# The turn from layer 0 to attention: tile 24's heads behind layer 0's last product, tile 25's in one piece, and the edge sums' bank emptied into a buffer of its own

## The chip, the core and the metric

One core of a Trainium2 chip. The metric is the device time of the whole program in microseconds (us), as the median of several runs. A second source is one profiled execution, read as a page and through questions to its trace. The engines are named as the profile names them: PE (TensorE's matmuls), PEld (its weight loads), DVE (VectorE), ACT (ScalarE), POOL (GpSimd), SP (SyncE, which issues most DMAs).

## What is computed

Two layers over a graph of 3327 nodes with 1024 features, in float32.

```python
# layer 0
h = max(layernorm(x), 0)
s = act_quant(relu(act_quant(h) @ weight_quant(w)))          # 4 bits
x = x + adj @ s                                               # scaled by asf and the quantisation steps
# layer 1
h = max(layernorm(x), 0)
Wh = einsum('nf,hfd->hnd', h, W)                              # 8 heads of 64
e = leaky_relu(Wh @ a1 [:, None] + Wh @ a2 [None, :], 0.2)
att = softmax(where(adj > 0, e, -9e15))
h = elu(att @ Wh)                                             # heads side by side: 512
out = relu(relu(relu(h @ W1.T + b1) @ W2.T + b2) @ W3.T + b3) @ W4.T + b4
x = x + out
```

## The kernel before

The nodes are padded to T = 26 tiles of 128 rows. Layer 0's second product (`mm`, line 726) takes each tile t of rows in four parts of 7, 6, 7 and 6 column blocks; every block of the adjacency is split into a high and a low float32r half (`hi` by ACT, line 185; `lo` by DVE, line 189) and multiplied with the resident quantised support `s_int[j]`. After a tile's product comes its chain: `y` (ACT, line 742; DVE, 744), `xt` = x + y (745), the row statistics (141 to 146), the ReLU of the centred row into `y` (144), its transpose into `ht`, and the inverse root `r` (`half_inverse`, lines 131 to 134, and 755).

`heads(t, ht, r)` makes layer 1's features of a tile: eight float32 products with `whead` (638; the profile counts 16 instructions), the scaled copy `wht` (ACT, 645), two products and reductions for `src` and `dst` (DVE, 652 and 653), exponentials on ACT (657, 676), the scaled features `ft` (DVE, 677), their high and low halves `fw` (ACT 692, DVE 693) and the halves `dw` that the edge sums use (ACT, 697). POOL stores them to `feat_d` (701) and `dsum_d` (705). In some tiles (`BATCHES`) the `src` rows gathered so far are transposed into the bank `sp` (661), copied (665) and stored to `src_d` (668). Heads of tile t - 1 are placed ahead of the last part of tile t's product. Tile t < 25 is transposed by DMA (`transposed_by_dma`, lines 607 to 612: two copies, two DMA transposes, two copies into `ht`); the last by TensorE (`transposed_by_tensor`, 626 and 627). With `own` given, `heads` also writes the first head's features straight into the attention's resident buffers `f_even` and `dw` (689, 691).

Attention sums over neighbours by two kinds of product. For each of 32 `attends` (column half, head pair, head, block group) and each of 26 neighbour tiles j, DVE makes a 0/1 selection `sel` (1063) of six or seven 128x128 blocks (which edges are on the positive side of the leaky ReLU), and PE adds `sel` times features into as many accumulator banks (`acc`, 1077). The second kind, the edge sums (`mps`, 852), multiplies the mask of one block (cast by ACT to `mf`, 13 tiles at a time, 849) with `dw` over all 26 tiles, in one bank, which ACT copies to `part` (856). `n` counts the pairs of attend and j; `edge_steps(n)` says how many edge products are done by then: before, none until n = 12, 24 at n = 14, all 338 of the first pair at n = 62.

The instructions of each engine run in the order that a scheduler lays down from priorities and estimated times. Three means fix it where wanted: `issue_after(ins)` puts a block's instructions of the same engine behind `ins`; `queue_behind(a, b)` puts a behind b; neither adds a wait. `keep_in_program_order` ties an instruction to the order of the source. Memory is reused: the eight PSUM banks of layer 0 (`mm` 4, `whm` 2, `sp` 1, `last` 1) become seven `acc` banks and one `mps` bank; the mask, features and `dw` of the attention lie where `s_int` lay, and its `sel`, `mf` and `srow` where `at`, `mk`, `hi` and `lo` lay.

The turn, as the trace before shows it: heads of tile 24 on PE from 899.4 to 906.1 us, the last 24 `mm` products to 912.13, then products of attend 0 for j = 0 to 3, the eight transposes of tile 25 (from 917.88), then tile 25's heads with one `acc` step (seven products) after each of their eight products (to 934.0), the transpose of `src`, 26 edge products, and the attention's steady order from about 950.

Of the kernel before, what the change touches and what calls it, by code (L numbers as in the profile page):

```python
# [8 lines left out]
F32 = mybir.dt.float32  # L9
# [36 lines left out]
BATCHES = {12: 0, T - 3: 13, T - 1: T - 2}  # L46
# [15 lines left out]
def two_layer_kernel(  # L62
# [105 lines left out]
    with tc.tile_pool(name="at", bufs=2, reuse_waits="tile") as atp:  # L168
# [419 lines left out]
        with tc.tile_pool(name="wh", bufs=1, reuse_waits="tile") as whp, tc.tile_pool(  # L588
# [31 lines left out]
            def transposed_by_tensor(y):  # L620
                ht = s2.tile([P, KF, P], F32, name="ht", bufs=1)
                for g in range(KF // 4):
                    tp = last_ps.tile([P, 4, P], F32, tag="last", name="tp2")
                    for q in range(4):
                        k = 4 * g + q
                        nc.tensor.transpose(tp[:, q, :], y[:, k * P : (k + 1) * P], ident)
                    last = nc.scalar.copy(ht[:, 4 * g : 4 * g + 4, :], tp)
                return ht, last

            def heads(t, ht, r, own=None):  # L630
                if t == T - 1:
                    whm, sp = (last_ps.tile([P, EMB], F32, tag="last", name=n) for n in ("whm", "sp"))
                else:
                    whm = wh_ps.tile([P, EMB], F32, name="whm")
                    sp = sp_ps.tile([P, EMB], F32, name="sp")
                of_k, products = [], []
# [9 lines left out]
                if t < T - 1:  # L646
# [10 lines left out]
                nc.scalar.activation(ratio[:, t], src, AF.Exp, scale=1.0 - SLOPE)  # L657
                if t in BATCHES:
                    first = BATCHES[t]
# [15 lines left out]
                for q, slope in enumerate((1.0, SLOPE)):  # L675
                    exps = nc.scalar.activation(ft[:, :, q, HD], dst, AF.Exp, scale=slope)
# [5 lines left out]
                if own is not None:  # L682
# [5 lines left out]
                    for up, value in zip(ups, values):  # L688
                        nc.scalar.copy(up, value)
                    for up, down, value in zip(ups, downs, values):  # L690
                        scaled = nc.vector.tensor_tensor(down, value, up.bitcast(F32), ALU.subtract)
                nc.scalar.copy(fw[:, :, 0], f2)
# [16 lines left out]
                return of_k, products, lows, exps, scaled, taken  # L709

            before = None
            for t in range(T):
# [5 lines left out]
                for js in PARTS:  # L718
                    hi, lo = part
                    part = next(columns, None)  # L720
                    if js is PARTS[-1] and before is not None:
                        _, products, lows, exps, made, _ = heads(*before)
# [18 lines left out]
                with tc.issue_after(exps.ins) if t == T - 1 else nullcontext():  # L741
                    nc.scalar.activation(y, mm, AF.Copy, scale=r_asf)
                with tc.issue_after(made.ins) if t == T - 1 else nullcontext():
# [499 lines left out]
```

## Time and profile before

| | us |
|---|---|
| Median of 3 runs | 2217.43 (2217.34 to 2218.85) |
| The profiled execution's own time | 2215.07 |
| Its span, first to last instruction | 2213.2 |
| PE busy | 2175.8 (98%) |
| DVE busy | 1541.5 (70%) |
| ACT busy | 1114.6 (50%) |
| Mean granted TensorE clock | 0.999 |

An instruction row gives start, duration, engine, line, operation, output and inputs, count, and in brackets the idle time of its engine before it with what ended that wait. A windows row gives the stretch, its length, the busy time of each engine with the number of instructions, the granted clock of TensorE (1.00 is full), the share of the DMA engines in use and the rate in GB/s. Of a duration of several matmuls in a row, the end is modelled.

### The profile page before, as it was taken

The numbers are of one execution on the slowest core, as the hardware profiler recorded it, in microseconds if no ns is written. First come the engines' busy times: TensorE is split into PE (matmuls) and PEld (weight loads), VectorE is DVE, ScalarE is ACT, GpSimd is POOL, SyncE is SP. The second block draws the span as 40 slices with busy tenths as digits, with TensorE's granted clock in tenths as the row PEclk, the third lists the DMA queues.
The fourth block names the chain that finished last, engine by engine and source line by source line (L and its number), as shares of the span: only waits on it lengthen the run. The fifth ranks groups of instructions, "written<-read, shape, count | busy, mean of one in ns | idle before, by whom it ended". The sixth has DMA issues, their size and how long they took to land.

```text
span 2213.2 us, 31276 instructions
## 1 busy us (share of the span) xinstructions
PE 2175.8 (98%) x12447; PEld 1749.6 (79%) x12457; DVE 1541.5 (70%) x1998; ACT 1114.6 (50%) x1714; POOL 176.8 (8%) x269
## 2 busy tenths in 40 slices
PE   5999999999999999999999999999999999999999
PEld 2477777777777777699999999999999999744444
DVE  8745555555455555678999999999999999822211
ACT  6734444544455544466556566565555555532110
POOL 2301000112001111000000000000000000000000
PEclk9999999999999999999999999999999999999999
DMA  6654566655556555934242432654242432372221
GB/s 219 166 185 156 158 189 184 177 166 158 182 185 185 168 168 160 332 117 149 87 148 80 132 101 60 217 162 145 87 150 87 138 90 78 100 205 92 95 86 67
DMA packets 242722, 321.40 MB, mean 145 GB/s; under 512 B 104901, under 2 KB 187285, under 8 KB 242577
## 3 DMA queue, kind: packets, MB, share of 16 engines
q1 hardware_dynamic: 221964, 246.18, 36.7%
q0 software_dynamic: 20544, 73.18, 10.5%
q8 instruction: 97, 1.59, 0.3%
q14 instruction: 49, 0.39, 0.1%
q10 hardware_dynamic: 68, 0.06, 0.0%
HBM read 208.99 MB, written 86.79 MB: 134 GB/s over the span
## 4 chain that ended last, share of the span: by engine, by line
PE 94%; DVE 3%; DMA 2%; ACT 1%; issue 1%; SPq 0%; POOL 0%; DVEq 0%; ACTq 0%; POOLq 0%
PE acc L1077 29%; PE mm L726 27%; PE mps L852 15%; PE whm L638 8%; PE o L1158 8%; PE h_ps L1118 5%; PE mm L337 2%; DMA xqt<-xq 0%; DVE stats L250 0%; DMA w<-in_w 0%; DVE sel L1063 0%; PE h_ps L1027 0%; PE o_half L1158 0%; DMA at<-in_adj_t 0%; DMA yht<-yh 0%
## 5 line engine op out<-in xcount | busy, mean ns | idle before, releaser
L1063 DVE SCALAR_TENSOR_TENSOR sel<-srow,ndst,mask 128x896 fp32r<-128x896 f32 (+1 forms) x832 | 864.0, 1078 | 51.6 <-PE acc L1077 40.2
L852 PE MATMUL mps<-dw,mf 128*128 128x260 f32 x2704 | 452.8, 283 | 0.3 <-ACT srct L665 0.3
L726 PE MATMUL mm<-s_int,hi 128*128 128x512 f32 x1352 | 426.7, 397 | 0.0
L726 PE MATMUL mm<-s_int,lo 128*128 128x512 f32 x1352 | 416.5, 389 | 0.0
L1077 PE MATMUL acc<-f_even,sel 128*128 128x260 f32 x2704 | 401.0, 286 | 2.9 <-DVE sel L1063 2.1
L1077 PE MATMUL acc<-f_odd,sel 128*128 128x260 f32 x2704 | 394.1, 286 | 0.4 <-DVE sel L1063 0.4
L849 ACT CAST mf<-mask 128x1664 fp32r<-128x1664 uint8 x208 | 331.3, 1593 | 118.8 <-PE mps L852 95.1
L852 PEld LDWEIGHTS mps<-dw,mf 128*128 128x128 f32 x2704 | 377.2, 188 | 1.1 <-ACT srct L665 0.6
L1077 PEld LDWEIGHTS acc<-f_even,sel 128*128 128x128 f32 x2704 | 356.8, 189 | 9.8 <-issue 3.6
L1077 PEld LDWEIGHTS acc<-f_odd,sel 128*128 128x128 f32 x2704 | 352.7, 188 | 7.9 <-issue 2.6
L726 PEld LDWEIGHTS mm<-s_int,hi 128*128 128x128 f32 x1352 | 254.0, 188 | 62.9 <-issue 12.0
L726 PEld LDWEIGHTS mm<-s_int,lo 128*128 128x128 f32 x1352 | 253.7, 188 | 52.8
L189 DVE TENSOR_TENSOR lo<-at,hi 128x896 fp32r<-128x896 f32 x104 | 106.2, 1021 | 130.4 <-ACT hi L185 130.2
L638 PE MATMUL whm<-whead,ht 128*128 128x512 f32 x416 | 183.8, 592 | 0.0
L1158 PE MATMUL o<-weights,h 128*128 128x512 f32 x400 | 174.8, 592 | 0.0
L190 DVE TENSOR_SCALAR mk<-at 128x896 uint8<-128x896 f32 (+1 forms) x104 | 61.5, 593 | 142.5 <-DMA at<-in_adj_t 142.5
L185 ACT CAST hi<-at 128x896 fp32r<-128x896 f32 x104 | 92.2, 887 | 134.7 <-PE mm L726 96.0
L1158 PEld LDWEIGHTS o<-weights,h 128*128 128x128 f32 x400 | 76.0, 190 | 94.4 <-issue 94.0
L638 PEld LDWEIGHTS whm<-whead,ht 128*128 128x128 f32 x416 | 78.3, 189 | 85.7 <-issue 83.5
L856 ACT COPY part<-mps 128x260 f32<-128x260 f32 x104 | 39.4, 379 | 188.4 <-PE mps L852 188.4
L921 POOL DMA_DIRECT2D enc_d<-eh x64 | 57.5, 903 | 934.2 <-ACT eh L919 933.7
L1128 ACT ACTIVATE h<-h_ps,rest 128x512 f32<-128x512 f32 (+1 forms) x54 | 34.8, 654 | 179.4 <-PE h_ps L1118 179.4
(169 smaller groups left out, 1674.1 us busy)
## 6 DMA issues: line engine op xcount, KB each, us to landing
feat_d<-fw POOLq DMA_DIRECT2D x26, 1040.0 KB, 5.4
f_even<-feat_d SPq DMA_DIRECT2D x7, 3380.0 KB, 13.5
f_odd<-feat_d SPq DMA_DIRECT2D x7, 3380.0 KB, 13.3
at<-in_adj_t SPq DMA_DIRECT2D x52, 448.0 KB, 4.4
at<-in_adj_t SPq DMA_DIRECT2D x52, 384.0 KB, 4.1
dw<-dsum_d SPq DMA_DIRECT2D x16, 910.0 KB, 9.2
dsum_d<-dw POOLq DMA_DIRECT2D x26, 520.0 KB, 6.4
x_d<-xt POOLq DMA_DIRECT2D x26, 512.0 KB, 6.7
```

The lines of the kernel that those rows point to most:

```text
L185: ins = nc.scalar.copy(hi, at)
L189: nc.vector.tensor_tensor(lo, at, hi.bitcast(F32), ALU.subtract)
L190: ins = nc.vector.tensor_scalar(mk[:, r], at, 0.0, None, ALU.is_gt)
L638: ins = nc.tensor.matmul(whm, ht[:, k, :], whead[:, k, :], start=(k == 0), stop=(k == KF - 1))
L726: nc.tensor.matmul(mm[:, c * 512 : (c + 1) * 512], which[:, q, :], s_int[j][:, c * 512 : (c + 1) * 512], start=(j == 0 and which is hi), s ...
L849: ins = nc.scalar.copy(mf, mask[:, j : j + TH, :])
L852: nc.tensor.matmul(ps, mf[:, j % TH, :], dw[:, j, :], start=(j == 0), stop=(j == T - 1))
L921: nc.gpsimd.dma_start(enc_d[q, sub[0] * P : (sub[-1] + 1) * P, h * HD : (h + 1) * HD].rearrange("(b p) d -> p b d", p=P), eh[:, q].rearran ...
L1063: ins = nc.vector.scalar_tensor_tensor(sel[:, :nb], srow[:, :nb], ndst[:, j, h : h + 1], mask[:, :, j, :], ALU.is_gt, ALU.mult,)
L1077: ins = nc.tensor.matmul(accs[b], sel[:, b, :], f[:, j, :], start=(j == 0), stop=(j == T - 1))
L1118: ins = nc.tensor.matmul(pss[m][:, :cols], wt[:, k, m * P : (m + 1) * P], xt[:, k, :cols], start=(k == 0), stop=(k == k_n - 1),)
L1158: nc.tensor.matmul(ps, h3[:, k, q * P : (q + 1) * P], w4[:, k, cs], start=(k == 0), stop=(k == D3 // P - 1),)
```

## The change

- Layer 0's last tile no longer has heads in front of its last part. `heads(24)` is called after the loop, with `own` buffers as `heads(25)` has; its products come after the last `mm` products, and its first DVE product and `wht` behind the end of tile 25's inverse root (`lacking`).
- Tile 25's two groups of transposes come behind the heads of tile 24, with attend 0's j = 0 between the groups and j = 1 to 3 behind the second; then all heads of tile 25 in one piece, then j = 4 to 7, then the edge products.
- On DVE `sel` 0 to 3 stand ahead of tile 25's y (`resumed`), 4 to 7 behind tile 24's scaled features, then tile 24's low halves, then tile 25's products; `sel` from 8 stands behind tile 25's scaled features.
- The edge sums begin at n = 7 with 24 steps at once and go on evenly from n = 9; the 338 are still reached at n = 62.
- The first edge block's bank is copied to `kept`, and from there to `part` before block 1's copy; the high copy `fw` of tile 25 stands behind that copy and behind the second mask cast of block 1.
- The `src` rows of tiles 24 and 25 are transposed in `last_src`, in the `mps` bank, after edge block 4.
- On SP the first half of the mask of group 0 and `srow` go ahead of the last DMA transpose of tile 24 (`turned`); the features and `dw` of tiles 20 to 23 go ahead of mask 1, tile 24 is no longer loaded for head 0.

```diff
-BATCHES = {12: 0, T - 3: 13, T - 1: T - 2}
+BATCHES = {12: 0, T - 3: 13}
...
             def transposed_by_tensor(y):
...
+                ends, copies = [], []
                 for g in range(KF // 4):
                     tp = last_ps.tile([P, 4, P], F32, tag="last", name="tp2")
...
+                    turns = [
+                        nc.tensor.transpose(tp[:, q, :], y[:, (4 * g + q) * P : (4 * g + q + 1) * P], ident)
+                        for q in range(4)
+                    ]
+                    ends.append((turns[0], turns[-1]))
+                    copies.append(nc.scalar.copy(ht[:, 4 * g : 4 * g + 4, :], tp))
+                return ht, ends, copies
...
-                    if js is PARTS[-1] and before is not None:
-                        _, products, lows, exps, made, _ = heads(*before)
+                    if js is PARTS[-1] and before is not None and t < T - 1:
+                        heads(*before)
...
+                resumed = nc.vector.tensor_scalar(y, y, asf_t, sup_delta, ALU.mult, ALU.mult)
...
+                lacking = nc.vector.tensor_scalar(r, r, 2.0, None, ALU.mult)
+                if t == T - 1:
+                    break
+                ht, turned = transposed_by_dma(y)
...
-            last_heads, *_, scaled, taken = heads(*before, own=(f_even, dw))
+            kept = large(early, "kept", [P, 2, 2 * HC])
+
+            of_k, products, lows, powers, scaled, own_lows, _, _, taken = heads(*before, own=(f_even, dw))
+            queue_behind(products[0], lacking)
+            queue_behind(taken, lacking)
+            ht, turns, copies = transposed_by_tensor(y)
+            queue_behind(turns[0][0], of_k[-1])
+            queue_behind(copies[0], taken)
+            queue_behind(powers[0], copies[-1])
+            last = heads(T - 1, ht, r, own=(f_even, dw))
+            queue_behind(last[1][0], lows)
...
-    FIRST = 12
+    FIRST = 7
...
-    YOUNG = 14
+    YOUNG = 9
...
+        def last_src():
+
+            first = max(BATCHES) + 1
+            n = (T - first) * NH
+            sp = m_ps.tile([P, 512], F32, tag="mps", name="sp2")
+            nc.tensor.transpose(sp[:n, :P], srcs[:, first:].rearrange("p t h -> p (t h)"), ident)
+            srct = s3.tile([P, P], F32, name="srct2")
+            nc.scalar.copy(srct[:n], sp[:n, :P])
...
+                            behind = nullcontext()
+                            if u == 0 and i * T + j <= T:
+                                behind = tc.issue_after((last[6] if i else powers)[-1].ins)
+                            with behind:
                                 ins = nc.scalar.copy(mf, mask[:, j : j + TH, :])
                             if amid:
-                                queue_behind(taken, ins)
+                                queue_behind(last[-1], ins)
+                            elif (u, i, j) == (0, 1, TH):
+                                queue_behind(last[7], ins)
...
+                            if u == i == 0:
+                                emptied.append(nc.scalar.copy(kept, whole))
+                                queue_behind(last[7], emptied[0])
+                            else:
+                                if (u, i) == (0, 1):
+                                    nc.scalar.copy(part[:, 0], kept)
+                                nc.scalar.copy(part[:, i % 7], whole)
...
+                    if (u, i) == (0, 4):
+                        last_src()
...
-        old, young = PARTS[:3], [range(20, 24), range(24, 25)]
+        old, young = PARTS[:3], [range(20, 24)]
+        ins = load_mask(0, SUBS[0], slice(0, TH))
+        with tc.issue_after(ins.ins):
+            srow, ins = load_src(0)
+        queue_behind(turned, ins)
         with tc.issue_after(turned.ins):
-            srow, ins = load_src(0)
...
             load_features(dw, dsum_d, 0, old)
+            load_features(dw, dsum_d, 0, young)
+            load_features(f_even, feat_d, 0, young)
             load_mask(1, SUBS[1])
...
-                ahead = ln if j < 14 else scaled
-                with tc.issue_after(ahead.ins) if i == 0 and j >= 4 else nullcontext():
+                behind = nullcontext()
+                if i == 0 and j >= 4:
+                    behind = tc.issue_after((scaled if j < 8 else last[4]).ins)
...
                 if i == 0 and j < 4:
-                    queue_behind(products[0], ins)
+                    queue_behind(resumed, ins)
+                elif i == 0 and j == 7:
+                    for later in (*own_lows, lows):
+                        queue_behind(later, ins)
+                elif i == 0 and j == 9:
+                    for later in last[5]:
+                        queue_behind(later, ins)
+                elif i == 0 and j == 14:
+                    queue_behind(last[2], ins)
+                behind = nullcontext()
+                if i == 0 and j < 18:
+                    behind = tc.issue_after(
+                        (turns[0][1], *[turns[1][1]] * 3, *[last[0][-1]] * 4, *summed * 10)[j].ins
+                    )
...
+                added[:] = [ins]
+                if i == 0 and j in (0, 3):
+                    queue_behind(turns[1][0] if j == 0 else last[0][0], ins)
```

## The prediction

> **What bounds the kernel now.** I read the page first (the shares, then the chain that ended last), then the windows around the turn from layer 0 to attention, then TensorE's timeline there, then the rows of ScalarE, VectorE and SP that end just before it.
>
> ```profile
> PE 2175.8 (98%) x12447; PEld 1749.6 (79%) x12457; DVE 1541.5 (70%) x1998; ACT 1114.6 (50%) x1714; POOL 176.8 (8%) x269
> PE 94%; DVE 3%; DMA 2%; ACT 1%; issue 1%; SPq 0%; POOL 0%; DVEq 0%; ACTq 0%; POOLq 0%
> ```
>
> TensorE is the bound: 37 us of idle time in 2213, most of it in the first 100 us. Only at the turn is there more to take:
>
> ```profile
> 900.00:910.00 10.00, 10.00 (x32) 5.77 (x31) 5.59 (x6) 1.97 (x2) 0.00 (x0) 1.00 1.06 370
> 910.00:920.00 10.00, 7.04 (x46) 5.82 (x44) 9.34 (x15) 4.43 (x9) 1.28 (x2) 1.00 1.09 355
> 920.00:930.00 10.00, 9.85 (x53) 7.22 (x54) 9.22 (x14) 4.93 (x5) 0.95 (x2) 1.00 1.04 395
> 930.00:940.00 10.00, 9.01 (x60) 7.37 (x58) 5.60 (x11) 3.53 (x9) 1.06 (x2) 1.00 0.92 331
> 940.00:950.00 10.00, 8.22 (x52) 7.71 (x51) 10.00 (x11) 4.97 (x6) 1.71 (x2) 0.83 0.64 194
> 950.00:960.00 10.00, 10.00 (x83) 9.80 (x83) 5.78 (x6) 6.51 (x6) 0.00 (x0) 1.00 1.06 314
> ```
>
> Columns: window, length, busy PE, PEld, DVE, ACT, POOL, granted PE clock, DMA share, GB/s. PE is full before 910 and after 950. Its timeline names each hole (in brackets):
>
> ```profile
> 913.36 2.55 PE L1077 MATMUL acc<-f_even,sel 128*128 128x260 f32 x19 [0.79 <-ACT y L742]
> 917.88 0.65 PE L626 MATMUL tp<-ident,y 128*128 128x128 f32 x4 [1.97 <-DVE y L144]
> ...
> 920.15 1.11 PE L1077 MATMUL acc<-f_even,sel 128*128 128x260 f32 x7 [0.28 <-DVE sel L1063]
> ...
> 936.31 0.27 PE L661 MATMUL sp<-ident,srcs 128*16 128x128 f32 x1 [0.65 <-DVE srcs L653]
> 936.92 3.57 PE L852 MATMUL mps<-dw,mf 128*128 128x260 f32 x26 [0.34 <-ACT srct L665]
> 941.17 1.11 PE L1077 MATMUL acc<-f_even,sel 128*128 128x260 f32 x7 [0.68 <-DVE sel L1063]
> 943.38 6.85 PE L1077 MATMUL acc<-f_even,sel 128*128 128x260 f32 x42 [1.10 <-DVE sel L1063]
> ```
>
> The seven holes sum to 5.81 us. The last row holds one more loss: 42 products took 6.85 us where the rate elsewhere (7 in 0.83 us) makes 5.00, so 1.85 us went to a clock that one-us windows show at 0.50 from about 943.8 to 947.2. All that this change can give is 5.81 + 1.85 = 7.7 us, as TensorE's work stays the same.
>
> **The change, part by part.** Times below are on the clock of this profile.
>
> 1. *Heads of tile 24 behind the last product.* Their 16 matmuls (899.2 to 906.07, 6.87 us) now stand behind the last 24 mm products, which end at 905.3 instead of 912.13. From there the chain y L742 1.11, L744 0.81, L745 1.23, statistics 1.29 and 0.21, L144 0.75 took 5.75 us with its gaps (912.13 to 917.88): y is ready at 911.0, while PE works on the heads until 912.1. The holes of 0.79 and 1.97 go. Were that cover gone, they would cost 2.76 again. The inverse root (Sqrt 0.20, four small DVE steps, 1.04 in all as at 892.0) ends near 912.3, as wht does not start before 912.15: costs nothing. Two of the three table loads (1.28 each at 907.4, 920.5, 934.7) fall away, since Sqrt now follows Sqrt and Exp follows Exp; the one left runs at about 914.9, where ScalarE has waited for it before.
>
> 2. *Turn of tile 25.* Transposes issue in 0.41 us a group; their copy is 0.59. Copy 0 stands behind wht (0.69), so it ends at 913.5, when PE has done group 0 and j=0 (0.83 us) and is at 913.4. One accumulator bank is also held until wht is read (912.85). Bounds 0 and 0.6; I take 0.3, near the row of 0.28.
>
> 3. *Heads of tile 25 in one piece.* j=1 to 3 (2.5 us), then 6.87 us of heads end at 923.4. Beneath them VectorE does tile 24: four product/reduce steps of 0.72 from 912.9 to 915.8, scaled features to 917.9, sel j=4 to 7 (4 x 1.08) to 922.2, the own lows and lows (0.5 + 1.24) to 924.0. wht of tile 25 comes at 924.1: VectorE is just in time. What was queued behind these waits are sels, ready before PE needs them.
>
> 4. *What is late next.* Tile 25's chain: wht 924.1, four steps to 927.0, exps and scaled to 928.55 (the same rows took 934.72 to 939.20), then sel j=8 to 929.75. PE covers it with j=4 to 7 (3.33) and 24 edge matmuls (2.88): it reaches j=8 at 929.55. Stall 0.2; j=9, whose sel follows at 1.08 spacing, another 0.2; two edge matmuls, then j=10 behind sel 10, which stands behind the own lows (0.5): 0.6. From j=11 PE needs 1.5 us a step (7 acc and 6 edge matmuls) and VectorE 1.1. Sum 1.05 (0 to 2.5), in place of 0.28 + 0.65 + 0.34 + 0.68 + 1.10 = 3.05.
>
> 5. *src of tiles 24 and 25 later.* Transpose (0.27), copy (0.26) and two POOL issues (1.06) move to block 4 of the edges, where the one mps bank is taken: 0.34 as at 936.92 if ScalarE is free, up to 1.6 if an mf cast (1.59) is in front, 0 if acc products are put between. I take 0.45. Its readers come half the attention later.
>
> 6. *kept, and the order on ScalarE.* One copy more (0.38) on an engine half idle: 0. It lets the edge bank be emptied before the high copy of tile 25 (1.06). That copy overwrites fw, so it waits for tile 24's store: issued near 924.3, and stores landed in 11.2 us at 919.3 (5.4 is the page's median). So it may wait to 935 with casts for block 2 behind it; those are wanted at about 939.9. 0, at worst 1.5.
>
> 7. *SP queue.* Seven mask loads (208 KB each) and srow (448 KB) move ahead of tile 24's last DMA transpose, so before xt of tile 25 too. Their space is free at 887.6. They pull 1.9 MB, 5.2 us at 370 GB/s, in front of it. Features of block 20 to 23 go ahead of mask1: dw, complete near 921 now, stays near 921, wanted at 926.7. xt lands near 903, wanted at 907.5. 0 for these.
>
> 8. *The cover that the last product loses.* Its last six blocks' hi and lo have had 6.87 us of heads in front; now PE wants them at 899.2:
>
> ```profile
> 889.79 4.47 SPq L609 DMA_TRANSPOSE yht<-yh  x2
> ...
> 895.38 1.35 ACT L612 COPY ht<-yht 128x1024 uint16<-128x1024 uint16 x1 [3.15 <-DMA yht<-yh]
> 896.60 0.82 ACT L185 CAST hi<-at 128x768 fp32r<-128x768 f32 x1
> 897.45 0.96 DVE L189 TENSOR_TENSOR lo<-at,hi 128x768 fp32r<-128x768 f32 x1 [4.39 <-ACT hi L185]
> ```
>
> lo ends at 898.4: 0.8 us to spare. hi stands behind a copy that waits for the transposes which part 7 delays. If ScalarE's order becomes hi first (its buffer is free at 893.0), nothing is lost; if not, every us of landing after 896.2 is a us of PE. DMA is full here (256 GB/s at a share of 1.09 from 890 to 900). The Trainium skill speaks against the change at this point: "DMA: Bandwidth & Descriptors", section "Queues, rings and completion order", says that one issuer's descriptors are consumed in ring order on each engine, and that an engine alternates between the queues. By that the transposes wait for the whole 1.9 MB and share with the stores: landing about 900.5, a stall of 4.3. By the row alone (landing in 5.6 us) it is 0. I take 0.3, as only loads issued before 889.8 precede the first transpose, and only the last one is tied behind srow.
>
> 9. *Clock.* The half clock followed 1.8 us of holes inside 3.4 us. In the new order the densest stretch (929.5 to 933) has 1.0 us. I take 0 for throttling, a gain of 1.85. "TensorE: Matmul & The Clock Gate", section "Why this matters for your kernels", asks only that no single gap pass about 3 us; the longest here is 1.97, so by the page these holes throttle nothing and the 1.85 need not come back. The trace, which shows it behind those holes, decides; by the page the sum is 3.7, by the trace 5.6.
>
> Sum: 5.81 + 1.85 - 0.3 - 1.05 - 0.45 - 0.3 = 5.6 us. The profiled execution (2215.07, span 2213.2) becomes 2209.5 (span 2207.6). It lies 2.4 us under the median of the runs; the same 5.6 from 2217.4 gives 2211.8, 0.25% less.
>
> **The rivals.** (a) *Part of the cover is missed*: the copy stays before hi and the transposes land between 897.5 and 900.5: 1.3 to 4.3 us back, 2213 to 2216. For it: DMA full, in-order queues. Against: only two of the moved issues need precede. (b) *The clock throttles anyway*: 2213.7. For it: the page; against it: the sparser holes. (c) *Slower*: the same place, further. If all eight loads precede both transposes and share with tile 23's stores (2.07 MB on the other queue), 4 MB at 367 GB/s from 887.6 end at 898.4, and the transposes' own 3 to 5 us land them near 904: hi waits, PE stands 7 us, 2219. The gain is gone from a landing at 901.8. (d) *Nothing happens*: the order is laid out differently and VectorE's chain for tile 25 keeps the same holes: 2215 to 2217.
>
> **How the numbers follow.** 0.2% (4.4 us) is about what a measurement of this kernel can tell from no change. Likeliest case 0.66, (a) 0.14, of which 0.04 stays beyond 0.2%, (b) 0.10, of which 0.02 does, (c) 0.07, (d) 0.03. Faster 0.72, same 0.21, slower 0.07. The range runs from all holes but 0.3 us closed, with 0.5 for the runs' spread (2209.6), to a stall of 4.3 in part 8 (2216.0).
>
> **What would show it.** Right: mm ends near 905.3, heads of 24 follow with no gap, transposes near 912.2, three small gaps (0.2 to 0.6) before j=8, 9, 10, clock 1.00 throughout, one table load between 905 and 935. Wrong: a PE wait on hi or lo at 899, a wait on wht before j=0, clock 0.50 near 930, or a wait of mps on ScalarE at block 4 above 1 us.

## The result, and the profile after

The changed kernel takes 2210.86 us (median of 8 runs, 2209.24 to 2212.9); the kernel before, measured with it, 2217.78 (8 runs, 2216.03 to 2218.85). The ratio is 0.9969, 95% interval 0.9958 to 0.998. The prediction said 2211.8. On a second chip the two gave 2210.43 (12 runs) and 2217.04 (16 runs), ratio 0.9973 (0.9964 to 0.9981). The profiled execution took 2210.92 us, its span is 2208.6, and its mean granted clock is 1.000 where it was 0.999.

The page's row of busy times and the row of engines under "chain that ended last" of the changed kernel:

```profile
PE 2173.7 (98%) x12457; PEld 1747.9 (79%) x12457; DVE 1542.5 (70%) x2000; ACT 1112.2 (50%) x1715; POOL 176.0 (8%) x269
PE 55%; DVE 1%; issue 0%; ACT 0%; DVEq 0%
```

TensorE is still the bound. The chain's shares add up to 56% only: it was followed back through that part of the span, so the second row is not to be set against the 94% of before. The work of TensorE is the same, so the gain has to stand in its idle time. The windows around the turn show it (window, length, busy PE, PEld, DVE, ACT, POOL, granted clock, DMA share, GB/s):

```profile
910.00:920.00 10.00, 10.00 (x50) 6.71 (x49) 8.21 (x18) 5.31 (x11) 0.55 (x1) 1.00 1.08 363
920.00:930.00 10.00, 10.00 (x54) 7.07 (x52) 8.50 (x13) 4.91 (x10) 1.67 (x2) 1.00 1.08 361
930.00:940.00 10.00, 9.26 (x74) 8.69 (x73) 10.00 (x12) 6.40 (x8) 0.00 (x0) 1.00 0.97 384
940.00:950.00 10.00, 8.60 (x72) 8.38 (x71) 7.80 (x8) 4.80 (x6) 1.66 (x2) 1.00 0.88 279
```

From 910 to 920, where before was busy for 7.04, TensorE is full; from 940 to 950 the clock is 1.00 where it was 0.83; and one loss is left there. TensorE's timeline names the three holes:

```profile
907.00 7.03 PE L641 MATMUL whm<-whead,ht 128*128 128x512 f32 x16
913.86 0.60 PE L627 MATMUL tp<-ident,y 128*128 128x128 f32 x4
...
932.22 2.17 PE L1132 MATMUL acc<-f_even,sel 128*128 128x260 f32 x14 [0.50 <-DVE sel L1107]
...
934.75 1.11 PE L1132 MATMUL acc<-f_even,sel 128*128 128x260 f32 x7 [0.25 <-DVE sel L1107]
...
941.30 1.01 PE L1132 MATMUL acc<-f_even,sel 128*128 128x260 f32 x7
943.71 1.11 PE L881 MATMUL mps<-dw,mf 128*128 128x260 f32 x7 [1.41 <-ACT part L895]
```

Neither the heads of tile 24 (907.00) nor the transposes behind them (913.86) carry a wait: the heads hide the whole chain over y, as the prediction's part 1 had it. The holes before j=8 and j=10 are those of part 4. The third, 1.41 us before the first edge product of block 2, is the one that the prediction put at nothing.

Two executions do not start alike, so I compare the turn by itself: the time from the start of the 3000th weight load to that of the 5000th (counted from 0; all 12457 are in every trace). It is 339.92 us before and 333.79 after, 6.13 less. The profiled pair, 2215.07 and 2210.92, differs by 4.15 only, since the changed kernel reached the 3000th load 1.77 us later (755.46 against 753.69). That is a matter of the execution: in the second chip's profile the same changed kernel reached it at 759.13. There the turn is 333.71, with the same waits, 1.4 and 0.7 us in sum.

One wait inside this stretch comes and goes between executions: TensorE's wait for the `src` terms of tile 23, near 880 us. It is 0.20 us in the profile of before, 0.28 in that of the changed kernel and absent from its second profile. So a difference of some 0.3 us between two turns can be chance.

### The profile page after: what moved, and what is told of

It reads as the page before. It is cut to its first block, busy times and chain, and to the rows that moved or that the text cites. A ratio compares the mean times of both kernels' runs of the same rounds, so it can differ in the third digit from the quotient of the medians.

```text
span 2208.6 us, 31285 instructions
## 1 busy us (share of the span) xinstructions
PE 2173.7 (98%) x12457; PEld 1747.9 (79%) x12457; DVE 1542.5 (70%) x2000; ACT 1112.2 (50%) x1715; POOL 176.0 (8%) x269
## 4 chain that ended last, share of the span: by engine, by line
PE 55%; DVE 1%; issue 0%; ACT 0%; DVEq 0%
PE acc L1132 28%; PE mps L881 14%; PE o L1214 8%; PE h_ps L1174 5%; DVE sel L1107 1%; PE o_half L1214 0%; ACT rest L1061 0%; DVE nodes L1199 0%; ACT su L937 0%; DVE su L941 0%; DVE su L934 0%; DVE yo L1203 0%; ACT h L1184 0%; ACT part L895 0%; DVE su L939 0%
```

## The experiments

Each run stands beside runs of the kernel before on its own chip: 2216.8 us for the first four, 2216.79 for the next four, 2216.39 for the two that alter the kernel before, 2217.04 for the last two. "Turn" is the stretch just defined, from the run's profile.

| kernel | median us (runs) | ratio to before, 95% | turn us |
|---|---|---|---|
| before | 2217.78 (8) | 1 | 339.92 |
| changed | 2210.86 (8) | 0.9969 (0.9958 to 0.998) | 333.79 |
| late_edges | 2212.35 (15) | 0.9979 (0.9971 to 0.9987) | 335.74 |
| eight_edges | 2210.61 (8) | 0.9972 (0.9962 to 0.9983) | 333.62 |
| bank_first | 2207.89 (4) | 0.9959 (0.9945 to 0.9974) | 331.79 |
| turned_first | 2211.12 (11) | 0.9978 (0.9969 to 0.9987) | 335.71 |
| wht_first | 2209.71 (6) | 0.9969 (0.9957 to 0.9981) | 333.17 |
| no_kept | 2216.83 (12) | 0.9999 (0.999 to 1.0007) | 340.06 |
| src_in_heads | 2210.41 (5) | 0.9971 (0.9959 to 0.9983) | 333.44 |
| three | 2207.84 (5) | 0.996 (0.9948 to 0.9973) | 331.22 |
| before_one | 2215.27 (13) | 0.9994 (0.9986 to 1.0002) | 339.22 |
| before_two | 2215.79 (13) | 0.9995 (0.9987 to 1.0004) | 339.57 |
| after_again | 2210.43 (12) | 0.9973 (0.9964 to 0.9981) | 333.71 |
| three_again | 2207.82 (5) | 0.996 (0.9946 to 0.9974) | 331.66 |

### late_edges: the edge products not before j=8

```diff
-    FIRST = 7
+    FIRST = 12
-    YOUNG = 9
+    YOUNG = 14
-                return min(max(0, n - FIRST) * START, START)
+                return min(max(0, n - FIRST) * 12, START)
-                        with tc.issue_after(added[0].ins) if (u, i, j) == (0, 1, 0) else nullcontext():
+                        with tc.issue_after(added[0].ins) if (u, i, j) in ((0, 0, 0), (0, 1, 0)) else nullcontext():
-                if i == 0 and j < 18:
+                if i == 0 and (j < 8 or (summed and j < 18)):
```

> The edge sums start at n = 12 again, as before the change (12 edge products after n = 12, 24 after n = 13), and the first is tied behind the acc products of its own step; all else as in the changed kernel. My theory: the 25 edge products are what covers tile 25's chain (wht, four product steps, exps, scaled, sel 8). Without them TensorE is through j = 7 at about 928.2 on the changed kernel's clock and waits for sel 8 until 932.2: a hole of 4.0 us instead of 0.5, then about 0.25 to 0.5 before each of j = 9 to 12, as a sel takes 1.08 us and its products 0.83: 5 to 6 us of holes where the changed kernel has 0.75, and half a window of 3.4 us at half clock after it (1.7 us). Time 2210.9 + 4.7 + 1.7 = about 2217, as the kernel before. Rival (the edge products are only moved, TensorE's sum of work is the same, the scheduler fills in other work): 2211, holes below 1.5 us. Rival on the clock (only a single gap above 3.4 us throttles): here it would throttle too.

TensorE's timeline, and below it windows of 3.41 us of TensorE alone (window, length, busy PE, granted clock, DMA share, GB/s):

```profile
931.52 5.99 PE L1132 MATMUL acc<-f_even,sel 128*128 128x260 f32 x35 [3.48 <-DVE sel L1107]
```

```profile
928.57:931.99 3.42, 0.47 (x3) 1.00 1.03 405
931.99:935.40 3.41, 3.41 (x18) 0.50 1.03 407
```

Without the 24 products the wait before j=8 is 3.48 us, and half a clock follows. Both were expected; but the turn is only 1.95 us longer than the changed kernel's, and the time lies between the two forecasts. The loss is paid back in part: this one wait is all that TensorE has at this turn, and the changed kernel's holes before j=10 and before block 2 are not in it. So the early edge products are worth 2 us of turn (2.3 if tile 23's wait, which this profile does not have, is taken off the changed kernel's), not the 3.5 of the hole that they fill and the half clock with it.

### eight_edges: 8 of the 24

```diff
-    START = T - 2
+    START = 8
-                        with tc.issue_after(added[0].ins) if (u, i, j) == (0, 1, 0) else nullcontext():
+                        with tc.issue_after(added[0].ins) if (u, i, j) in ((0, 0, START), (0, 1, 0)) else nullcontext():
```

> 8 instead of 24 edge products at n = 7, the ninth tied behind the acc products of its own step, the rest spread evenly to n = 62. This tests the clock. Hole before j = 8: 0.5 + 17 x 0.119 = 2.5 us, then at most 0.25 before j = 9: no single gap above 3 us, but 2.5 to 2.7 us of idle time inside one window of 3.4. Theory from the profile of the kernel before (1.78 us idle of 3.4 were followed by half clock, 1.4 us were not): a half clock window of 3.4 us follows in most executions, and costs 1.7 us. Time 2210.9 + 2.0 + 1.7 = 2214.6. Rival (a throttle needs one gap of about 3 us or more): clock 1.00 through the turn, time 2212.9.

One hole of TensorE, and none behind it:

```profile
930.87 2.17 PE L1132 MATMUL acc<-f_even,sel 128*128 128x260 f32 x14 [2.52 <-DVE sel L1107]
```

The turn is 333.62, that of the changed kernel within 0.2. The changed kernel's three holes add up to 2.16, this single one to 2.52. Both forecasts of time, 2214.6 and 2212.9, were missed: they kept the changed kernel's hole before block 2, and here it is gone. TensorE's order explains it. Between the last edge product of block 1 and the first of block 2 (948.33) it has 36 accumulation products in this run, and only seven in the changed kernel (941.30 above):

```profile
943.99 4.50 PE L1132 MATMUL acc<-f_even,sel 128*128 128x260 f32 x36
```

These cover the copy that empties the bank. So what 16 more products hide before j=8 comes back as the hole before block 2: moving this work by itself was worth nothing more.

### bank_first: the bank of block 1 emptied before kept is copied and before the next mask cast

```diff
+                            elif (u, i, j) == (0, 2, TH):
+                                queue_behind(ins, emptied[1])
...
+                                copied = nc.scalar.copy(part[:, i % 7], whole)
                                 if (u, i) == (0, 1):
-                                    nc.scalar.copy(part[:, 0], kept)
-                                nc.scalar.copy(part[:, i % 7], whole)
+                                    emptied.append(copied)
+                                    queue_behind(nc.scalar.copy(part[:, 0], kept), copied)
```

> ScalarE copies block 1's bank to part ahead of the second mask cast of block 2, and moves kept to part only after that. In the changed kernel TensorE waits 1.41 us at block 2's first edge product because the mask cast (1.58) and the copy from kept (0.40) stand in front of the copy that empties the bank. Theory: the hole falls to 0.2 or less, with its 0.2 of restart: gain 1.4 us, 2209.5. Rival (part's memory is not free until the low halves of tile 25 are done near 940.1, or later): the bank copy waits instead, the hole stays or grows: 2210.9 to 2213.

ScalarE's timeline, first in the changed kernel:

```profile
941.50 1.58 ACT L874 CAST mf<-mask 128x1664 fp32r<-128x1664 uint8 x1 [0.44 <-PE mps L881]
942.98 0.40 ACT L894 COPY part<-kept 128x260 f32<-128x260 f32 x1
943.29 0.37 ACT L895 COPY part<-mps 128x260 f32<-128x260 f32 x1
```

and then in bank_first:

```profile
940.06 0.38 ACT L895 COPY part<-mps 128x260 f32<-128x260 f32 x1 [0.24 <-PE mps L883]
940.33 0.41 ACT L898 COPY part<-kept 128x260 f32<-128x260 f32 x1
940.64 1.58 ACT L874 CAST mf<-mask 128x1664 fp32r<-128x1664 uint8 x1
```

The changed kernel empties the bank third, behind a cast of 1.58 and the copy of kept, while TensorE waits; here it does so as soon as the bank is full. All that the waits view of TensorE then names at the turn is

```profile
PE acc L1135 <- DVE sel L1110: 0.7, 2, 0.5
```

(us in total, times, longest). The 1.41 us are gone, which shows the cause of the third hole. The turn is 2.00 us shorter, where the forecast was 1.4. TensorE's rows at the place of the hole say why:

```profile
939.86 1.01 PE L1135 MATMUL acc<-f_even,sel 128*128 128x260 f32 x7
940.71 1.00 PE L883 MATMUL mps<-dw,mf 128*128 128x260 f32 x7
```

From start to start this is 0.85 us; in the changed kernel it is 2.41 (941.30 to 943.71), and the seven edge products behind the hole take 1.11 instead of 1.00. So the hole cost 1.56 + 0.11 = 1.67, which is 0.26 more than its bracket: the bracket begins only at the modelled end of the product before. The other 0.33 of the 2.00 are the wait for tile 23's `src` terms, which this profile does not have.

### turned_first: SP issues tile 24's transposes ahead of the masks and srow, as before

```diff
-        ins = load_mask(0, SUBS[0], slice(0, TH))
-        with tc.issue_after(ins.ins):
-            srow, ins = load_src(0)
-        queue_behind(turned, ins)
         with tc.issue_after(turned.ins):
+            srow, ins = load_src(0)
+        with tc.issue_after(ins.ins):
+            ins = load_mask(0, SUBS[0], slice(0, TH))
+        with tc.issue_after(ins.ins):
```

> The order on SP as before the change: both DMA transposes of tile 24, then xt, srow and the first half of mask 0. Theory: the transposes land near 897.2 on the changed kernel's clock instead of 898.8, hi and lo of the last blocks are 1.5 us earlier (gain at most 0.2 us, what TensorE now loses there), but the mask lands near 906, sel 0 to 3 end near 910.5 and tile 25's y, queued behind them on VectorE, starts 2 us later than 908.4: the chain to the transposes passes its cover by about 1 us. Time 2210.9 + 0.8 to 1.5 = about 2212. Rival (the loads ahead of the transposes only cost, as the mask is not wanted so early): 2210.7, and no hole before the transposes.

TensorE's timeline, then VectorE's:

```profile
915.75 0.66 PE L627 MATMUL tp<-ident,y 128*128 128x128 f32 x4 [1.89 <-DVE lnv L146]
```

```profile
906.96 4.34 DVE L1107 SCALAR_TENSOR_TENSOR sel<-srow,ndst,mask 128x896 fp32r<-128x896 f32 x4 [6.92 <-DMA mask<-mask_d]
911.22 0.81 DVE L746 TENSOR_SCALAR y<-y,every,sup_delta 128x1024 f32<-128x1024 f32 x1
```

The first four masks become sels only at 906.96, when the bytes are there; the change has queued the second step of y of tile 25 behind them on VectorE, where it begins at 911.22; the chain outlasts the heads of tile 24 by 1.89 us, where about 1 was forecast. The turn is 1.92 longer. So the reordered SP queue is part of what hides the chain: with the heads moved and the queue as it was, the cover of part 1 is not complete.

### wht_first: wht of tile 25 ahead of tile 24's first halved sums

```diff
-                    nc.scalar.copy(
+                    halved = nc.scalar.copy(
...
+            queue_behind(halved, last[-1])
```

> Asks about part 3 of the prediction. In the changed kernel the scaled copy of the last tile's heads' product (wht of 25) began 0.7 us after its product ended, because a copy of tile 24's halved sums (the first half of dw, L701, 0.63 us) stood ahead of it on ScalarE; VectorE's chain up to the mask of j=8 then ran late, and TensorE stood 0.50 us before j=8. Here that one copy is put behind wht of 25. Theory (the copy ahead of wht is what made j=8 late): wht begins at its product's end, the hole before j=8 falls from 0.50 to 0.1 or nothing, and the turn, between the 3000th and the 5000th weight load, falls from 333.8 to about 333.2 us; time 2210.2, 0.5 to 0.7 below the changed kernel. Rival (VectorE, not wht, is what j=8 waits for: it ends the low parts of tile 24 at about 926 anyway): the hole stays at 0.4 to 0.5 and so does the time, 2210.9. A second way to lose: the halved sums of tile 24 now leave later, their DMA holds back the same copies of tile 25, and the last rows of dw land late; then a new wait before the last edge products of block 1, over 1 us.

ScalarE's timeline in the changed kernel, where the copy of the halved sums is in front, and then TensorE's in wht_first:

```profile
925.41 0.63 ACT L701 CAST dw<-fw 128x520 fp32r<-128x520 f32 x1 [2.24 <-DVE fw L697]
925.94 0.68 ACT L648 ACTIVATE wht<-whm,lnr 128x512 f32<-128x512 f32 x1
```

```profile
930.31 1.12 PE L1133 MATMUL acc<-f_even,sel 128*128 128x260 f32 x7
932.84 1.11 PE L1133 MATMUL acc<-f_even,sel 128*128 128x260 f32 x7 [0.25 <-DVE sel L1108]
941.86 1.11 PE L882 MATMUL mps<-dw,mf 128*128 128x260 f32 x7 [1.44 <-ACT part L896]
```

j=8 (930.31) shows no wait any more; the other two holes stay; the turn is 0.62 shorter. The theory is right in the trace about the hole. But some 0.3 of the 0.62 are tile 23's wait, which this profile does not have, so the order itself is worth rather 0.3 than the forecast 0.6. The ratio, 0.9969, cannot show so little.

### no_kept: block 0's bank copied straight into part

```diff
-                            elif (u, i, j) == (0, 1, TH):
-                                queue_behind(last[7], ins)
...
-                                emptied.append(nc.scalar.copy(kept, whole))
-                                queue_behind(last[7], emptied[0])
+                                nc.scalar.copy(part[:, 0], whole)
                             else:
-                                if (u, i) == (0, 1):
-                                    nc.scalar.copy(part[:, 0], kept)
                                 nc.scalar.copy(part[:, i % 7], whole)
```

> Asks what the separate copy of block 0's edge sums (kept) is worth. Here block 0's bank is copied straight into part, as every other bank is, and kept is gone, with the two orders on ScalarE that hung on it. part's memory comes free only when tile 25's features are done with, so the bank of block 0 is held until then and block 1's edge products cannot start. Theory: the changed kernel frees the bank at about 934 us of its trace, here it comes free at 940 or later; until then only accumulations of j=8 and on are left for TensorE, each of which needs a mask from VectorE that is busy with the features, so TensorE waits in several pieces: 1.5 to 4 us on top of the changed kernel, 2212.4 to 2215, and the 1.41 us hole before block 2's first edge product may stand elsewhere. Rival (the accumulations have masks enough, and part is free early enough): no loss, and since ScalarE has one copy less before block 2's bank, a gain of up to 0.4; 2210.5 to 2210.9.

TensorE's timeline, then ScalarE's:

```profile
940.74 2.32 PE L879 MATMUL mps<-dw,mf 128*128 128x260 f32 x9 [5.87 <-ACT part L888]
```

```profile
935.35 1.06 ACT L696 CAST fw<-ft 128x1040 fp32r<-128x1040 f32 x1 [4.70 <-DMA feat_d<-fw]
...
939.80 0.62 ACT L701 CAST dw<-fw 128x520 fp32r<-128x520 f32 x1
940.33 0.36 ACT L888 COPY part<-mps 128x260 f32<-128x260 f32 x1
```

The bank is held until tile 25's halved sums are done at 940.4, and these wait for tile 24's store of the features, which lands at 935. TensorE stands 5.87 us in one piece, and its granted clock is 0.50 from 938.4 to 945.2. The turn is 340.06: everything that the change gained is gone. My direction was right, my size (1.5 to 4) too small: the accumulations that could have filled the hole stand behind block 1's edge products in TensorE's own order, so having masks for them did not help. The copy of 0.38 us that part 6 puts at 0 carries, with its two orders, the whole gain of the rest. The run removes the two orders on ScalarE together with the copy, so it does not tell what each is worth.

### src_in_heads: the transpose of the src terms back in tile 25's heads

```diff
-BATCHES = {12: 0, T - 3: 13}
+BATCHES = {12: 0, T - 3: 13, T - 1: T - 2}
-                    sp = sp_ps.tile([P, EMB], F32, name="sp")
+                    if t == T - 1:
+                        sp = last_ps.tile([P, EMB], F32, tag="last", name="sp")
+                    else:
+                        sp = sp_ps.tile([P, EMB], F32, name="sp")
-                    if (u, i) == (0, 4):
-                        last_src()
```

> Asks what moving the transpose of the last tiles' attention source terms out of the heads (last_src) is worth. Here tile 25's heads make it again where the kernel before did, behind the sums that give src, in a bank of the turn; last_src is gone, the rest is the changed kernel. Theory: TensorE meets the transpose in its queue shortly after the last tile's heads' product and waits there for VectorE's sums over wht, which end later than in the kernel before since VectorE makes masks j=4 to 7 first; the wait is 0.3 to 1.5 us, of which the 0.50 us before j=8 is part, since VectorE gets on meanwhile; +0.2 to +1.0, 2211.1 to 2211.9. Rival (the transpose lies behind products that cover it, and only its 0.1 us counts): 2210.9, same as the changed kernel, and moving it was worth nothing.

TensorE's timeline:

```profile
927.92 0.27 PE L668 MATMUL sp<-ident,srcs 128*16 128x128 f32 x1 [0.34 <-DVE srcs L656]
```

The transpose waits 0.34 us before j=7, and the 0.50 before j=8 is gone with it, since VectorE got on meanwhile. The turn is 0.35 shorter than the changed kernel's, not longer, and those 0.35 are no more than tile 23's wait, which this profile does not have. So last_src is worth nothing here; the 0.99 that this step cost before (0.65 and 0.34) was won by what lies beside it, not by moving it.

### before_one and before_two: the kernel before with more masks ahead of the last features

```diff
-                ahead = ln if j < 14 else scaled
+                ahead = ln if j < 15 else scaled        # before_one; 16 in before_two
```

> Asks whether the half clock of the kernel before (one stretch of 3.41 us at 0.5 from 943.8) hangs on the two holes of 0.68 and 1.10 us just ahead of it. The kernel before, with one mask more (j=14) made ahead of the last tile's features on VectorE, which stands idle for 3.8 us there; nothing of the turn is moved. Theory (a stretch in which TensorE stands for about half is followed by one at half clock): the hole of 0.68 before j=14 goes, that of 1.10 before the next stays at 0.4 to 1.1, the stretch ahead has 1.1 us idle or less, as other stretches of the kernel before that were followed by full clock; so no half clock: 0.7 + 1.7 = about 2.4 us, 2214.4 against 2216.8 before. Rival (the clock follows all the standing of the turn, 5.81 us, not one stretch): the half clock stays and only the hole goes, 2216.1.

> The same with two masks more (j=14 and 15) ahead of the features. Theory: both holes, 0.68 and 1.10, go, no stretch at half clock follows: 1.78 + 1.7 = about 3.5 us, 2213.3; against the run with one mask the difference is the second hole alone, up to 1.1. Rival (clock follows the turn's sum): 1.8 and 2215.0. Third case (the features, made later by up to 1.1 us, hold back the rows of the last tile for the accumulation of its own j or the copy of the bank): a new wait of 0.5 to 1 further on.

These ask about the half clock alone. Windows of the length of the stretch that ran at half clock, laid end to end from a change of the granted clock. First the kernel before:

```profile
916.52:919.93 3.41, 1.92 (x13) 1.47 (x13) 3.34 (x6) 1.14 (x3) 0.66 (x1) 1.00 1.11 361
940.41:943.83 3.42, 1.64 (x11) 1.35 (x11) 3.42 (x4) 3.42 (x5) 1.25 (x2) 1.00 0.10 8
943.83:947.24 3.41, 3.41 (x18) 3.41 (x17) 3.41 (x4) 1.14 (x2) 0.47 (x1) 0.50 0.92 240
```

Then before_one:

```profile
941.90:945.32 3.42, 1.63 (x12) 1.38 (x12) 3.42 (x4) 3.42 (x5) 1.28 (x2) 1.00 0.14 20
945.32:948.73 3.41, 3.41 (x18) 3.41 (x17) 3.41 (x4) 1.10 (x2) 0.43 (x1) 0.50 0.91 232
```

And before_two:

```profile
916.40:919.82 3.42, 1.34 (x12) 1.13 (x11) 3.32 (x6) 0.50 (x1) 0.55 (x1) 1.00 1.10 354
919.82:923.23 3.41, 3.41 (x18) 3.41 (x17) 3.41 (x5) 1.84 (x4) 1.69 (x2) 0.50 1.07 378
943.71:947.12 3.41, 2.31 (x16) 1.93 (x17) 3.41 (x4) 3.41 (x5) 1.72 (x2) 1.00 0.33 71
```

Both forecasts of time failed, for a reason that the windows show. In before_one the holes of 0.68 and 1.11 did not close: one mask more for TensorE only made it wait one mask further on. As in the kernel before, where the window ahead of the half clock is 1.78 us idle, they lie in one window, 1.79 us idle, and half clock follows. In before_two one of them shrinks to 0.29 and falls into the window ahead; the late window has 1.10 us idle and full clock follows. But in that execution the windows lie otherwise over the early holes (1.39 and 2.08 instead of 0.79 and 1.97): one has 2.08 us idle, and half clock follows, where the kernel before had at most 1.49 idle in a window there, and full clock (916.52 to 919.93). So the half clock goes with the idle time of one window, not with the sum over the turn, and where windows begin is not tied to the kernel's work.

What half clock costs a run stands in the runs of before_two: the three whose mean clock was 1.000 have a median of 2213.85 us, the seven with 0.999 2215.79, the three with 0.998 2217.09, so 3.2 us over two steps. In the four sets of runs of the kernel before the two steps come to 2.1 to 3.0 us. That is 1.0 to 1.6 us a step; half of 3.41 is 1.7, and a step of the rounded mean need not be just one stretch.

### three: bank_first, wht_first, and the high part of the last mm operand before the copy of the transposed tile

```diff
+            queue_behind(joined_up[-2], casts[-1])
+            queue_behind(halved, last[-1])
+                            elif (u, i, j) == (0, 2, TH):
+                                queue_behind(ins, emptied[1])
...
+                                    queue_behind(nc.scalar.copy(part[:, 0], kept), copied)
```

> The changed kernel with three ScalarE orders at once: the bank of block 1's edge sums is emptied ahead of the kept copy and of the mask cast (which alone took the 1.41 us hole away and gave 2207.9), wht of 25 is put ahead of tile 24's first halved sums (the 0.50 us hole before j=8), and the high part cast of the last mm operand ahead of a copy of the transposed tile. Theory (the holes are separate and add up): the holes left in the turn are 0.3 us or less in all, the turn is 331.1 us or so against 331.8 of the bank's order alone, time 2207.3. Rival (they share a cover: VectorE is what the accumulations wait for, and what one order gives another takes): 2207.9, not below the bank's order alone, with a hole of 0.4 or more still before j=8 to 10.

```profile
PE acc L1141 <- DVE sel L1116: 0.2, 1, 0.2
```

That is all that the waits view of TensorE has left at the turn. The turn is 2.57 us shorter than the changed kernel's and 0.57 shorter than bank_first's; the medians, 2207.84 and 2207.89, cannot tell these two apart.

### after_again and three_again: the changed kernel and the three orders on one chip

> The changed kernel itself, unedited, on the same chip as the three orders together, since the two were so far measured beside different runs of the kernel before. Theory (the holes seen in its profile are in every execution): it lies 5.5 to 7 us below the kernel before, and 2.2 to 2.8 us above the kernel with the three orders, whose turn is 2.57 us shorter in the profile. Rival (the two differ in one execution only): the medians are within 1 us of each other.

> The three orders together once more, unedited, beside the changed kernel. Theory: 2.2 to 2.8 us below the changed kernel on this chip, about 2207.5 where before is 2216.6. Rival: within 1 us of it. The profile should again show one hole of 0.2 to 0.3 us in the turn and no others.

2210.43 against 2207.82: the three orders take 2.6 us off the changed kernel on the same chip, as their turn said. The kernel with them beats both. In the second profile its turn is 331.66, of which 0.31 is tile 23's wait; neither bank_first nor the first profile has it. Without it the step over bank_first is 0.4 to 0.6 us.

## Why the prediction was right, and where it was not

The prediction took 5.6 us off the profiled execution and off the median. The turn gave 6.13, and the medians differ by 6.9.

- **Part 1**, heads of 24 as cover: right. 0.79 and 1.97 are gone; mm ends near 907, which is the 905.3 forecast plus the later start of this execution; one table load is left. turned_first shows that the cover needs part 7's order too.
- **Part 2**, the turn of tile 25: about 0.25 where 0.3 was put, though no bracket shows it. The copy of the first group was done before j=0 was, but j=0 itself was slow:

```profile
914.06 0.69 ACT L648 ACTIVATE wht<-whm,lnr 128x512 f32<-128x512 f32 x1 [0.88 <-PE whm L641]
914.22 1.33 PE L1132 MATMUL acc<-f_even,sel 128*128 128x260 f32 x7
914.81 0.39 PE L1132 MATMUL acc<-f_even,sel 128*128 128x260 f32 x1
```

Its seven products take 1.17 us to the next row (915.39), and seven elsewhere 0.83 (936.77 to 937.60); 0.08 of the difference is only that the first of them starts early behind a transpose. One of the seven (the third row, taken by itself) starts at 914.81, 0.06 after ScalarE has read wht out of its bank. So the prediction's second reason, the bank held until wht is read, fits; no run tests it by itself.
- **Parts 3 and 4**, VectorE just in time and holes at j=8, 9, 10: 0.50, 0, 0.25, sum 0.75 in brackets instead of 1.05. The 0.2 before j=8 became 0.50 because of a queue that the prediction did not follow: the halved sums of tile 24 on ScalarE, ahead of wht (wht_first).
- **Part 5**, last_src: 0 instead of 0.45. Twelve accumulation products lay over its copy.
- **Part 6**, ScalarE's order: the mis-sized term, 1.41 us in its bracket and 1.67 in fact where 0 was put and 1.5 was the bound, and in another place. The prediction looked at the casts for block 2; TensorE waited for the copy that frees the bank, behind one of those casts and behind the copy of kept (bank_first). And kept was costed at 0 without the price of its absence, which is 6.3 us of turn (no_kept).
- **Part 7**: 0, right.
- **Part 8**, hi and lo: 0.1 instead of 0.3 (0.2 in the second profile). The transposes landed at 898.8, on before's clock 0.8 later than the limit that the prediction set, and ScalarE kept the bad order; yet the lo products started hardly late. In the kernel before and in the changed one:

```profile
899.61 7.03 PE L638 MATMUL whm<-whead,ht 128*128 128x512 f32 x16
```

```profile
901.46 0.61 PE L730 MATMUL mm<-s_int,hi 128*128 128x512 f32 x2
901.92 0.70 PE L730 MATMUL mm<-s_int,lo 128*128 128x512 f32 x2
```

The limit was 0.85 us too early: TensorE comes to this place at 899.61, not at 899.2, and the two hi products that go first give lo 0.45 more. The estimate of a 4.3 us stall, worked out from the page "DMA: Bandwidth & Descriptors" of the Trainium skill, section "Queues, rings and completion order", did not come true, since it took all eight loads to precede the transposes: the profile has the first transpose issued behind three masks (893.83), and its copy starts 5.0 us later, where it took 5.6 before. The page's ring order is neither shown nor refuted by that.
- **Part 9**, clock: right for the profiled pair; no window at half clock is left in the turn. As a term of the medians it is less sure, since not every execution of the kernel before pays it: of its 29 runs beside the first four experiments, 4 had clock 1.000 (median 2215.7), 17 had 0.999 (2216.68) and 8 had 0.998 (2217.8). The mean counts half clock anywhere in the program, so it is no measure of the turn alone: the changed kernel's second profile has 0.998 from stretches at 34.92 and 546.92 us, far from the turn.

Holes closed, by their brackets: 5.81 - 2.16 = 3.65; with the clock's 1.85 it is 5.50. The turn gave 0.6 more. bank_first shows where it lies: a hole between accumulation and edge products costs more than its bracket says. The other runs agree, taken from start to start: 2.80 for the bracket of 2.52 in eight_edges, 3.76 for 3.48 in late_edges. (After the heads' product it is less: turned_first opened a hole of 1.89 for 1.92.) If each start is set against the spacing that its kind of product has elsewhere, the turn before loses about 8.0 us to waits and 1.6 to the clock, and the changed kernel's 3.5 to waits. That makes 6.1, the whole of the gain. The clock's term is 1.6 here because the prediction's 1.85 sets a row with its modelled end against a rate without one: from 943.38 the next row starts at 950.07, 6.69 later and not 6.85, and 0.1 of what is left belongs to the hole in front.

So the mechanism of the prediction held, but that its sum came so near is partly luck. Parts 4, 5 and 8 were together 0.95 us too cautious, and the holes that went cost about 0.9 more, net, than their brackets, against the 1.41 that part 6 missed.

Of the rivals, (a) and (c) fell with part 8, (b) with the clock, (d) with part 1.

## What to carry to other kernels

A cover that moves from one place to another is worth what the next late resource leaves of it: here 16 products more before j=8 were worth nothing until one bank's copy was put first on ScalarE. When an engine at half load feeds the one that bounds, walk its queue instruction by instruction at the place in question; the order of a few small copies was worth 2.6 us, beside 6.9 for the whole change. And cost a small buffer by what happens without it, not by its copy. Where a tenth of a microsecond counts, measure a hole from start to start, beside the same place without the hole.

## What was not expected of the hardware

The granted clock changes at the bounds of windows of 3.413 us that follow each other without regard to the kernel: in the second profile of the changed kernel two stretches at half clock begin at 34.92 and 546.92 us, which is 150 times 3.413 apart. At the turn, windows at full clock with 1.78 us of TensorE idle (before), 1.79 (before_one), 2.08 (before_two), 2.95 (late_edges) and 3.42 (no_kept) were followed by one at half clock; those with up to 1.60 idle were not. In eight_edges a hole of 2.52 fell as 1.60 and 0.92 into two windows, and the clock stayed full in the profiled execution. It is the same far from the turn. In the changed kernel's second profile, TensorE stands 1.84 us in one window for tile 12's `src` terms:

```profile
543.51:546.92 3.41, 1.57 (x8) 1.00 (x7) 2.34 (x4) 1.17 (x3) 0.55 (x1) 1.00 0.22 88
546.92:550.34 3.42, 3.42 (x10) 2.67 (x9) 2.35 (x5) 0.46 (x3) 2.99 (x6) 0.50 0.20 69
```

Near 31 us, windows with 1.62 (three) and 1.63 idle (late_edges and the same second profile) were followed by half clock too. So in these traces the limit lies at about 1.6 us of 3.41, a little under half a window. One window with 1.89 idle was not followed by half clock (turned_first; what ran in the rest of it was the float32 heads' product). So it is not idle time alone, and how the kinds of product count stays open.

The page "TensorE: Matmul & The Clock Gate" of the Trainium skill calls the window free-running in its Part 1 and gives it 3413 ns, with which the 3.413 us agree. Its advice in "Why this matters for your kernels", no gap over about 3 us, is not enough here: the two gaps ahead of the kernel before's half clock were 0.68 and 1.10.
